# One more quarter product in six matrices, left sums kept in DRAM, a cast moved to VectorE, and pauses on GpSimd, in a relational graph layer

## The chip, the cores and the metric

One Trainium2 core of one chip. The metric is device microseconds of a whole launch; the median of three launches is given, and one further launch was profiled. TensorE is PE, VectorE is DVE, ScalarE is ACT, GpSimd is POOL and SyncE is SP, as the profile names them.

## The reference

1250 nodes with 1024 features, 20,000 edges with a source, a destination and one of 8 relations, everything in float32:

```
h   = relu(layernorm(x))
u   = h @ root + bias + sum_r mean_r(h[src], by dst) @ weight[r]
z   = concat([u, h]) @ w_gate + b_gate
out = x + tanh(u) * z + h * (1 - z)
```

`mean_r` averages over the edges of relation r that end in a node. All matrices are 1024 x 1024, and `w_gate` is two of them.

## The kernel before

**Order of the work.** The kernel multiplies first and gathers afterwards: for each of 11 matrices (s = 0 to 7 the relations, 8 the root, 9 the half of `w_gate` that takes h, 10 the half that takes u) TensorE multiplies h by the matrix. The products of the relations go to DRAM (`y`), those of matrices 8 and 9 to `hr_dram` and `z_dram`. The gather of edge rows from `y`, with a scaled addition for each (`add_slot`: GpSimd issues an indirect DMA into one of five `got` buffers, VectorE adds it to `u` with its weight), runs beside later products: those of relations 0 to 4 beside matrices 5 to 7, the rest beside matrices 8 and 9. Beside matrices 0 to 4 run the layer norm, and then an index that sorts the edges by destination: counting with one-hot matmuls, a table in DRAM that GpSimd fills by one indirect scatter for each 128 edges (`scatter`), and an order of the nodes. Matrix 10 comes last, by itself, with the gate's arithmetic.

**One product.** The 1250 rows are 10 blocks of 128, taken as 5 entries (i = 0 to 4) of two blocks (d = i and i + 5). An entry and a matrix are both cut into 2 x 2, and `product` forms them by Strassen's scheme in Winograd's form: seven products of 512 x 512 factors (`p1` to `p7`) in place of eight. `h_op[i]` holds the seven left factors (A11, A12, A22, S1 to S4), and `Factors` the seven right ones (B11, B21, B22, T1 to T4), of which VectorE makes four by `make_t1` to `make_t4`. One of the seven products is four matmuls of 512 columns for an entry; two entries need eight of them.

**Quarter products.** Entries 0 and 1, and entries 2 and 3, are taken together (`paired`). For such a pair, some of the seven products are again done by the same scheme, one level down: seven products of two matmuls of 256 columns each, in place of eight matmuls of 512 columns. There is a class for each: `First` (A11 B11), `Second` (A12 B21), `Third` (S4 B22) and `Fifth` (S1 T1). `First` and `Second` are used for matrices 1 to 9, `Third` for matrices 4 to 9 (`thirds`, `EARLY = 3`), and `Fifth` for matrices 1 to 4 (`fifths`, `FIFTHS = (1, 4)`); for matrices 5 to 9 S1 T1 is done whole, in `p5`. The sums that the quarter products need are VectorE's. `First`, `Third` and `Fifth` share one place for their sums (`room`, named `inner` in the profile), so `sums` (the factors s1, t1, s2, t2) and `next_sums` (four more in their place) have to wait until TensorE has read what lies there. `Second` has room of its own in the buffers that the matrix before has left free (named `w`): `left` and `next_left` make its four left sums from h, which are the same for every matrix, and `right` its right ones.

**What sets the order.** The schedule is written by hand: each engine does its instructions in the order in which the code gives them out. `product` calls `between(j)` after each of its parts, and `step` uses these calls to hang sums, loads and the work beside (`beside`, `sums`, `early`, `fill`) into the order. `fill` names what comes after which part. With `Fifth`, an even entry begins with `root.begin()` (a11 b11), then `first.late()`, `root.sums()`, `root.second()`, the whole product S2, `root.early()`, `root.next_sums()`, and, inside `p7`, the whole product S3, `between(TICK)` and `root.late()`. `spread` gives the steps of the gather out in proportion to a count that every `between` call raises by a number that depends on the entry.

**Memory.** PSUM has eight banks: four named `ps` in turn, two `ps_b`, one `ps_n`, one `ps_q`. `sum_bank(odd)` gives `ps_n`, or one `ps` bank that is kept for as long as `Fifth` is in use (three are then left to take turns); a matmul by `ident` writes a kept bank once before its first use. SP and ACT issue the loads and stores of matrices and rows; SP's instructions wait in their order too.

**Index.** In `slots`, each round of four times 128 edges passes `one_hots`, `count`, `add_counts`, and then splits the running counts into two bf16 parts: `as_bf16` (a cast, ScalarE) and `residue` (VectorE), which `look` multiplies.

Of the kernel before, what the change touches and what calls it, by code (L numbers as in the profile page):

```python
# [9 lines left out]
F32 = mybir.dt.float32  # L10
BF16 = mybir.dt.bfloat16
# [10 lines left out]
def tile_rgcn_highway(  # L22
# [31 lines left out]
    nc = tc.nc  # L54
# [3 lines left out]
    P = 128  # L58
# [6 lines left out]
    H = Q // 2  # L65
# [7 lines left out]
    EARLY = 3  # L73
# [5 lines left out]
    CG = 4  # L79
# [2 lines left out]
    UB = 4  # L82
    LATE = 4
    TICK = 9
    FIFTHS = (1, 4)
    IDLE = 12

# [18 lines left out]
    dram = ctx.enter_context(tc.tile_pool(name="dram", bufs=1, space=bass.MemoryType.DRAM))  # L106
# [11 lines left out]
    table = dram.tile([G * KEYS * SLOTS, 1], I32, name="table")  # L118
    table_more = dram.tile([G * KEYS * MORE, 1], I32, name="table_more")
    edges_dram = dram.tile([3, P, NCH], F32, name="edges_dram")  # L120
    val_dram = dram.tile([G, KEYS], F32, name="val_dram")
    node_dram = [dram.tile([KEYS, 1], I32, name=f"node_dram{g}") for g in range(G)]

    narrow, kept = [False], []

    def bank():
        return psum.tile([P, 512], F32, name="ps", bufs=4)

    def sum_bank(odd):

        if odd:
            if not kept:
                kept.append(bank())
                nc.tensor.matmul(kept[0].rearrange("p (c k) -> p c k", c=CG), ident,
                                 ident[:, None, :].to_broadcast([P, CG, P]), start=True, stop=True)
            return kept[0]
        return psum.tile([P, CG, P], F32, name="ps_n", bufs=1).rearrange("p c k -> p (c k)")

# [63 lines left out]
    class Second:  # L202
# [3 lines left out]
        def __init__(self, f, i):  # L206
            b = f.place["b21"]
            f0, f1 = [t.rearrange("p k n -> p (k n)") for t in f.spare]
            self.b11, self.b12, self.b21, self.b22 = [
                b[:, k:k + 2, c:c + H] for k in (0, 2) for c in (0, H)]  # L210
            self.t1, self.t2, self.t3, self.t4 = [
                f0[:, k * Q:(k + 1) * Q].rearrange("p (k n) -> p k n", k=2) for k in range(4)]
            self.s1, self.s2, self.s3, self.s4 = [
                f1[:, k * H:(k + 1) * H].rearrange("p (k n) -> p k n", k=2) for k in range(4)]
            self.p1_p6, self.p5, self.p7 = f1[:, 2 * Q:3 * Q], f1[:, 3 * Q:3 * Q + H], \
                f1[:, 3 * Q + H:]
            self.a11, self.a12, self.a21, self.a22 = [
                h_op[i + o][:, A12, k:k + 2] for o in (0, 1) for k in (0, 2)]

        def right(self, k):  # L220
            to, a, b = ((self.t1, self.b12, self.b11), (self.t2, self.b22, self.t1),
                        (self.t3, self.b22, self.b12), (self.t4, self.b21, self.t2))[k]
            nc.vector.tensor_sub(to, a, b)

        def left(self):
            nc.vector.tensor_add(self.s1, self.a21, self.a22)
# [248 lines left out]
    def product(aop, w, to, between=lambda j: None, last=None, pieces=1, whole=True,  # L475
# [38 lines left out]
        def p7():  # L514
# [3 lines left out]
            if root and head:  # L518
                between(TICK)
                root.late()  # L520
# [132 lines left out]
    fac = []  # L653
# [7 lines left out]
    def thirds(s):  # L661

        return s > EARLY
# [2 lines left out]

        return s > 0

    def fifths(s):

        return FIFTHS[0] <= s <= FIFTHS[1]

    waiting, waiting_third, waiting_first, waiting_fifth = {}, {}, {}, {}
    at_call = [0, 0]
# [9 lines left out]
    def step(s, i, between=lambda j: None, second=None):  # L684

        two = paired(s, i)
        narrow[0] = fifths(s)
        if not narrow[0]:
            kept.clear()
        if (s, i) == (NM - 2, NP - 1):  # L690
# [4 lines left out]
            t.reverse()  # L695
        if two and i % 2 == 0:
            waiting[i] = Second(fac[s], i), t[0]
            if fifths(s):
                waiting_fifth[s, i] = Fifth(fac[s], i, room, p5_room)

        def put(i, part, t):
# [11 lines left out]
        def beside(j):  # L713
            at_call[:] = i, j
            new = fac[s + 1]
            if i == 0 and s > 0 and j == 1:
                fac[s].make_t4()
            if two and i == 0:
                sums(j)
            if two and i % 2 == 0 and j == 3:  # L720
                if not root:
                    waiting_first[s, i].fifth_to()
                if i == 0:
                    waiting[0][0].left()
                if q:
                    q.sums()
            if q and i % 2 and j == 1:
                q.next_sums()
                q.first_to(to[:, Q:])
            if q and i % 2 and j == 3:  # L730
                q.fifth_to(t[0][:, Q:])
            if coming and (i > 1 or not q) and j == 2:
                first_sums()
            if two and (i, j) == (1, 6):
                Second(fac[s], 2).left()
                Second(fac[s], 2).next_left()
            if (s, i, j) == (0, 0, 3) or (s > 0 and (i, j) == (3, int(thirds(s) or fifths(s)))):
                new.load_first()
            if (s, i, j) == (0, 0, 3) or (s > 0 and (i, j) == (3, 2)):
                new.load_next()  # L740
            if i == NP - 1:
                if j == 0:
                    new.load_b22()
                elif j == 1:
                    new.make_t1()
                elif j == 3:
                    new.load_b21()
                elif j == 4:
                    new.make_t2()
                elif j == 5 and not coming:  # L750
                    new.make_t3()
                elif j == 6 and coming:
                    new.make_t3()
            between(j)

        def sums(j):


            e = waiting[0][0]
            for k in {2: (0, 1), 5: (2, 3)}.get(j, ()) if s > EARLY else (j,) if j < 4 else ():  # L760
                e.right(k)
            if j == (5 if s > EARLY else 4):
                e.next_left()

        coming = next_first(s, i)
        root = waiting_fifth.get((s, i - i % 2)) if two else None
# [11 lines left out]
        if two:  # L778
            e, to = waiting[i - i % 2]
# [73 lines left out]
    nc.tensor.matmul(sum_bank(0).rearrange("p (c k) -> p c k", c=CG), ident,  # L853
                     ident[:, None, :].to_broadcast([P, CG, P]), start=True, stop=True)
# [12 lines left out]
    apart = const.tile([P, 1], F32, name="apart")  # L867
# [76 lines left out]
    with ExitStack() as early:  # L944
# [230 lines left out]
        def scatter():  # L1175

            if placed:
                c0, c1, at, over, where = placed.pop(0)
                of = slice(c0 - at, c1 - at)
                nc.vector.scalar_tensor_tensor(at_i[:, c0:c1], over[:, of], float(FAR),  # L1180
                                               where[:, of], op0=OP.mult, op1=OP.add)
                for c in range(c0, c1):
                    n = nedges(c)
                    ins = nc.gpsimd.indirect_dma_start(  # L1184
                        out=table[:, :],
                        out_offset=bass.IndirectOffsetOnAxis(ap=at_i[:n, c:c + 1], axis=0),
                        in_=row_col[:n, c:c + 1], in_offset=None,
                        bounds_check=G * KEYS * SLOTS - 1, oob_is_err=False)
                    tc.declare_no_dep(ins.ins, query=no_wait, group="scatter", reason="each edge has its own slot")
                    tc.add_to_no_dep_group("scatter", ins.ins)  # L1190

        def slots(ix):

# [3 lines left out]
            seen = ix.tile([P, RING, NHI], F32, name="seen", bufs=1)  # L1197
# [290 lines left out]
        while going[0]:  # L1488
            s, i = next(steps)
# [11 lines left out]
    with ExitStack() as edges_part:  # L1501
# [89 lines left out]
        def spread(e, total, parts):  # L1591

            said = [0, 0]
            parts *= 10

            def between(j):
                said[0] += (10, 8, 13, 11, 8)[at_call[0]]
                while said[1] < min(total, -(-total * said[0] // parts)):
                    next(e, None)
                    said[1] += 1  # L1600
                if said[0] == parts:
                    for _ in e:
                        pass

            return between
# [45 lines left out]
        s, i = next(steps)  # L1651
        while s <= EARLY:
            step(s, i)
            s, i = next(steps)
# [90 lines left out]
        while s < R0[1]:  # L1745
            step(s, i, on)
            s, i = next(steps)
# [14 lines left out]
        s, i = beside(first_group, sum(K[0]) + LATE + 1, s, i, R0[2] - 1)  # L1762
# [4 lines left out]
        with tc.If(passes > 0):  # L1767
# [15 lines left out]
            p = Passes()  # L1783
# [125 lines left out]
        while s < NM - 1:  # L1909
# [8 lines left out]
            s, i = next(steps, (NM, 0))  # L1918
# [86 lines left out]
```

## Time and profile before

| | before |
|---|---|
| time of three launches, us | 1330.55, 1331.38, 1331.61 (median 1331.38) |
| the profiled launch, us | 1331.68 |
| its span in the profile, us | 1329.9 |
| PE, DVE, ACT, POOL busy, us | 1315.0, 1028.2, 279.5, 579.2 |
| DMA moved | 263.75 MB, mean 198 GB/s |

The span is what the profile covers; the launch's time is 1.8 us more. Busy time is a sum over the instructions of an engine. A float32 matmul shows as two records in the trace, so that a group of four matmuls has the count x8. A row of the chain of waits gives a start, a length and what ran.

### The profile page before, as it was taken

Reading aid. Unit: us, or ns where it says so; the run is one execution under the profiler, and the core shown is the slowest. Engines: PE = TensorE matmul, PEld = TensorE weight load, DVE = VectorE, ACT = ScalarE, POOL = GpSimd, SP = SyncE. Lnnn points to the kernel's source line nnn. Section 1 sums busy time; section 2 is a strip of 40 time slices with the busy share of each in tenths; the row PEclk is TensorE's granted clock in tenths of the full one; section 3 lists DMA queues with packets and bytes.
Section 4 is the critical chain, followed back from the end, with each engine's and each line's share of the span. In section 5 each row is a group of like instructions: output and inputs, shape, how many; then the busy total and the mean of one; then the engine's idle time right before and its main releaser. Section 6 shows DMA issues by size and latency. Waiting matters only on the chain.

```text
span 1329.9 us, 13668 instructions
## 1 busy us (share of the span) xinstructions
PE 1315.0 (99%) x4212; PEld 734.2 (55%) x4212; DVE 1028.2 (77%) x2132; ACT 279.5 (21%) x547; POOL 579.2 (44%) x510
## 2 busy tenths in 40 slices
PE   9999999999999999999999999999999999999997
PEld 5444565556455546655655655565465556544443
DVE  6768977797784676558977988897788799867974
ACT  3352122122112212211221211121122112122210
POOL 0001546454655047401453546446265555715631
PEclk9999999999999999999999999999999999999999
DMA  8976355734834252144648769778788957969961
GB/s 306 302 228 165 87 96 129 155 60 77 161 103 101 81 115 49 53 159 153 221 138 305 254 236 368 261 256 275 250 280 304 353 180 246 323 249 292 326 178 60
DMA packets 116802, 263.75 MB, mean 198 GB/s; under 512 B 33150, under 2 KB 44818, under 8 KB 116592
## 3 DMA queue, kind: packets, MB, share of 16 engines
q1 hardware_dynamic: 56528, 112.62, 28.4%
q0 software_dynamic: 44064, 118.20, 28.1%
q10 hardware_dynamic: 16128, 31.98, 7.9%
q8 instruction: 33, 0.54, 0.2%
q14 instruction: 49, 0.40, 0.1%
HBM read 202.34 MB, written 75.41 MB: 209 GB/s over the span
## 4 chain that ended last, share of the span: by engine, by line
PE 81%; issue 6%; DMA 5%; DVE 5%; POOL 2%; SPq 1%; ACT 1%; POOLq 0%; DVEq 0%
PE ps_b L491 39%; PE ps L235 16%; PE ps L491 11%; PE ps_n L491 5%; PE ps_b L235 3%; PE ps_n L235 2%; DMA got<-y,idx 2%; PE ps_q L235 2%; PE ps_q L491 2%; DMA xt<-in_x_dram 1%; POOL got L1533 1%; DMA w<-in_L_gnn_weight_dram 1%; DVE u L1538 1%; POOL out_dram L878 0%; DVE h_op L472 0%
## 5 line engine op out<-in xcount | busy, mean ns | idle before, releaser
L491 PE MATMUL ps_b<-w,h_op 128*128 128x512 f32 x1464 | 659.1, 594 | 1.0 <-ACT row L595 0.8
L491 PEld LDWEIGHTS ps_b<-w,h_op 128*128 128x128 f32 x1464 | 274.4, 190 | 305.0 <-issue 294.2
L1533 POOL DMA_INDIRECT got<-y,idx x193 | 248.2, 1286 | 285.9 <-DVE u L1538 184.1
L1538 DVE SCALAR_TENSOR_TENSOR u<-got,w_of,u 128x1024 f32<-128x1024 f32 (+1 forms) x193 | 246.8, 1281 | 40.6 <-DMA got<-y,idx 38.1
L1184 POOL DMA_INDIRECT table<-row_col,at_i x157 | 172.6, 1099 | 154.6 <-DVE at_i L1180 109.0
L491 PE MATMUL ps<-w,h_op 128*128 128x512 f32 (+1 forms) x432 | 192.1, 586 | 0.8 <-ACT row L569 0.8
L491 PEld LDWEIGHTS ps<-w,h_op 128*128 128x128 f32 x432 | 81.1, 190 | 91.5 <-issue 85.9
L491 PE MATMUL ps_n<-w,h_op 128*128 128x512 f32 x208 | 94.4, 593 | 0.0
L235 PE MATMUL ps<-inner 128*128 128x256 f32 x360 | 91.6, 380 | 0.3 <-DVE inner L290 0.3
L235 PE MATMUL ps<-w,h_op 128*128 128x256 f32 x320 | 83.0, 382 | 1.0 <-ACT w L252 1.0
L235 PEld LDWEIGHTS ps<-inner 128*128 128x128 f32 x360 | 67.8, 190 | 18.6 <-issue 9.0
L517 ACT COPY row<-ps_b 128x512 f32<-128x512 f32 x53 | 31.0, 585 | 218.2 <-PE ps_b L491 218.2
L235 PEld LDWEIGHTS ps<-w,h_op 128*128 128x128 f32 x320 | 59.9, 190 | 28.8 <-issue 20.2
L595 ACT COPY row<-ps_b 128x512 f32<-128x512 f32 x54 | 31.6, 585 | 205.1 <-PE ps_b L491 205.1
L235 PE MATMUL ps<-w,w 128*128 128x256 f32 x288 | 70.8, 380 | 0.5 <-ACT w L241 0.5
L235 PEld LDWEIGHTS ps<-w,w 128*128 128x128 f32 x288 | 54.3, 190 | 20.1 <-issue 13.4
L491 PEld LDWEIGHTS ps_n<-w,h_op 128*128 128x128 f32 x208 | 39.3, 190 | 45.1 <-issue 44.2
L523 DVE TENSOR_TENSOR row<-row 128x512 f32<-128x512 f32 x44 | 30.2, 686 | 44.0 <-ACT row L517 42.5
L639 ACT COPY row<-ps_b 128x512 f32<-128x512 f32 x40 | 23.4, 585 | 175.8 <-PE ps_b L491 142.7
L1299 DVE SCALAR_TENSOR_TENSOR junk<-k_bc,key_col,before 128x128 f32<-128x128 int16 x157 | 54.8, 349 | 4.2
L552 ACT COPY row<-ps_b 128x512 f32<-128x512 f32 x54 | 31.7, 587 | 83.5 <-PE ps_b L491 76.1
L448 POOL MEMSET h_op<- 32x1024 f32 x1 | 0.9, 946 | 97.1 <-DVE rs L986 97.1
(254 smaller groups left out, 1539.9 us busy)
## 6 DMA issues: line engine op xcount, KB each, us to landing
y<-row SPq DMA_DIRECT2D x72, 512.0 KB
w<-in_L_gnn_weight_dram ACTq DMA_DIRECT2D x21, 1024.0 KB
w<-in_L_gnn_weight_dram SPq DMA_DIRECT2D x10, 1024.0 KB
w<-in_L_gnn_w_gate_dram ACTq DMA_DIRECT2D x6, 1024.0 KB
k_bc<-keys_dram SPq DMA_DIRECT2D x39, 128.0 KB
l_bc<-los_dram SPq DMA_DIRECT2D x39, 128.0 KB
h_dram<-h_op SPq DMA_DIRECT2D x9, 512.0 KB
u<-in_L_gnn_bias_dram SPq DMA_DIRECT2D x9, 512.0 KB
```

The lines of the kernel that those rows point to most:

```text
L235: nc.tensor.matmul(p, a[:, k, :], b[:, k, :], start=(fresh and k == 0), stop=(k == 1), skip_group_check=True)
L448: nc.gpsimd.memset(to[n // 32 * 32:], 0.0)
L491: nc.tensor.matmul(b[:, at], aop[:, i, k, :], w.of[i][:, k, at], start=(fresh and k == 0), stop=(k == KQ - 1), skip_group_check=True)
L517: nc.scalar.copy(d, b)
L523: nc.vector.tensor_add(c22, c if lone else c22, d)
L552: nc.scalar.copy(c11, b)
L595: nc.scalar.copy(c12, b)
L639: nc.scalar.copy(c21, b)
L1184: ins = nc.gpsimd.indirect_dma_start(out=table[:, :], out_offset=bass.IndirectOffsetOnAxis(ap=at_i[:n, c:c + 1], axis=0), in_=row_col[:n, ...
L1299: nc.vector.scalar_tensor_tensor(junk, o["k_bc"][:, i, :], key_col[:, c:c + 1], before, op0=OP.is_equal, op1=OP.mult, accum_out=rank[:, c: ...
L1533: nc.gpsimd.indirect_dma_start(out=t[:n], out_offset=None, in_=y[g][:, :], in_offset=bass.IndirectOffsetOnAxis(ap=at[:n, d, k:k + 1], axis=0),
L1538: nc.vector.scalar_tensor_tensor(u[:n], t[:n], w, u[:n], op0=OP.mult, op1=OP.add)
```

## The change

- `fifths(s, i)` is true for every matrix from 1 on, so `Fifth` is used in matrices 5 to 9 as well. The whole product S1 T1 of entries 0 to 3 goes in these, and the kept `ps` bank stays kept up to the end of matrix 9.
- The left sums of `Second` are made in matrix 1 alone, and stored to `lefts_dram` (one DMA of 512 KB for each pair of entries). From matrix 2 on SP loads them: for entries 0 and 1 at `(0, 0)`, for entries 2 and 3 at `(1, 6)`.
- `as_bf16` is a `tensor_copy` of VectorE in place of a copy of ScalarE.
- After each scatter into the table GpSimd does three memsets of one column (`apart`).
- `touch`, which writes a kept bank first, reads the identity as bf16, and stands ahead of eleven small matmuls at the start (before: eight small ones, then a float32 one).
- `spread` doesn't count the `TICK` call of entries other than 0, so that its sum stays what it was.

```diff
-    FIFTHS = (1, 4)
+    LEFTS_AT = 6
...
+    def touch(b):
+        of = ident.bitcast(BF16)[:, :P]
+        nc.tensor.matmul(b.rearrange("p (c k) -> p c k", c=CG), of,
+                         of[:, None, :].to_broadcast([P, CG, P]), start=True, stop=True)
...
-                nc.tensor.matmul(kept[0].rearrange("p (c k) -> p c k", c=CG), ident,
-                                 ident[:, None, :].to_broadcast([P, CG, P]), start=True, stop=True)
+                touch(kept[0])
...
+        def keep_lefts(self):
+            s, of = self.lefts()
+            nc.sync.dma_start(of, s)
+
+        def load_lefts(self):
+            s, of = self.lefts()
+            nc.sync.dma_start(s, of)
...
-    def fifths(s):
-        return FIFTHS[0] <= s <= FIFTHS[1]
+    def fifths(s, i=0):
+        return s > 0
...
-                if i == 0:
+                if i == 0 and s == 1:
                     waiting[0][0].left()
...
-            if two and (i, j) == (1, 6):
+            if two and (i, j) == (1, 6) and s == 1:
                 Second(fac[s], 2).left()
                 Second(fac[s], 2).next_left()
+                Second(fac[s], 2).keep_lefts()
+            if two and s > 1 and (i, j) == (0, 0):
+                waiting[0][0].load_lefts()
+            if two and s > 1 and (i, j) == (1, LEFTS_AT):
+                Second(fac[s], 2).load_lefts()
...
-            if j == (5 if s > EARLY else 4):
+            if s == 1 and j == 4:
                 e.next_left()
+                e.keep_lefts()
...
-    for _ in range(IDLE - CG):
+    touch(sum_bank(0))
+    for _ in range(IDLE - 1):
         nc.tensor.matmul(bank()[:, :P], ident, ident, start=True, stop=True)
...
                     tc.add_to_no_dep_group("scatter", ins.ins)
+                    for _ in range(3):
+                        nc.gpsimd.memset(apart, 0.0)
...
-                        nc.scalar.copy(s_b[:, to:to + n, 0], seen[:, k:k + n])
+                        nc.vector.tensor_copy(s_b[:, to:to + n, 0], seen[:, k:k + n])
...
-                said[0] += (10, 8, 13, 11, 8)[at_call[0]]
+                if j != TICK or at_call[0] == 0:
+                    said[0] += (10, 8, 13, 11, 8)[at_call[0]]
```

More of the change, by code (lines that the diff above doesn't have):

```diff
@@ L120, in tile_rgcn_highway @@
     edges_dram = dram.tile([3, P, NCH], F32, name="edges_dram")
+    lefts_dram = dram.tile([2, P, 4 * H], F32, name="lefts_dram")
     val_dram = dram.tile([G, KEYS], F32, name="val_dram")
@@ L214, in __init__ @@
                 f1[:, k * H:(k + 1) * H].rearrange("p (k n) -> p k n", k=2) for k in range(4)]
+            self.i, self.s_all = i, f1[:, :4 * H]
             self.p1_p6, self.p5, self.p7 = f1[:, 2 * Q:3 * Q], f1[:, 3 * Q:3 * Q + H], \
@@ L223, in right, with lefts @@
             nc.vector.tensor_sub(to, a, b)
+        def lefts(self):
+            return self.s_all, lefts_dram[self.i // 2]
+        def keep_lefts(self):
[4 more added lines that the diff above has]
+            nc.sync.dma_start(s, of)
         def left(self):
@@ L686, in step @@
         two = paired(s, i)
-        narrow[0] = fifths(s)
+        narrow[0] = fifths(s, i)
         if not narrow[0]:
@@ L697, in step @@
             waiting[i] = Second(fac[s], i), t[0]
-            if fifths(s):
+            if fifths(s, i):
                 waiting_fifth[s, i] = Fifth(fac[s], i, room, p5_room)
@@ L849, in tile_rgcn_highway @@
     make_identity(nc, ident)
-    for _ in range(IDLE - CG):
+    touch(sum_bank(0))
+    for _ in range(IDLE - 1):
         nc.tensor.matmul(bank()[:, :P], ident, ident, start=True, stop=True)
-    nc.tensor.matmul(sum_bank(0).rearrange("p (c k) -> p c k", c=CG), ident,
-                     ident[:, None, :].to_broadcast([P, CG, P]), start=True, stop=True)
     eps = const.tile([P, 1], F32, name="eps")
```

## The prediction

> **What bounds the kernel now.** I read the totals of the page first, then the table of stages, then TensorE's waits, then VectorE's waits stage by stage, and last the chain of waits. The totals (engine, busy us, share):
>
> ```profile
> PE 1315.0 (99%) x4212; PEld 734.2 (55%) x4212; DVE 1028.2 (77%) x2132; ACT 279.5 (21%) x547; POOL 579.2 (44%) x510
> ```
>
> A busy PE can hide waits, so I look for them stage by stage. Each row is one stretch: its bounds, its length, then busy us of PE, PEld, DVE, ACT, POOL, the granted clock, and the DMA share. I cut them near the matrices' borders; the rows are matrices 2, 4, 5, 7 and 8.
>
> ```profile
> 266.00:388.00 122.00, 121.25 (x475) 69.95 (x475) 97.80 (x390) 25.02 (x65) 69.74 (x61) 1.00 0.53 108
> ...
> 505.00:614.00 109.00, 109.00 (x357) 66.89 (x356) 67.21 (x145) 21.71 (x45) 32.91 (x31) 1.00 0.26 80
> 614.00:730.00 116.00, 116.00 (x354) 66.39 (x353) 98.00 (x153) 20.82 (x42) 53.34 (x44) 1.00 0.66 225
> ...
> 846.00:962.00 116.00, 115.65 (x352) 66.11 (x352) 95.18 (x121) 20.82 (x42) 53.92 (x46) 1.00 0.78 263
> 962.00:1078.00 116.00, 116.00 (x353) 66.38 (x352) 96.10 (x128) 20.83 (x42) 66.60 (x52) 1.00 0.88 307
> ```
>
> PE fills every stage at clock 1.00. VectorE has 18 to 21 us free in each of matrices 5 to 9, and 42 us in matrix 4, which already has the layout that matrices 5 to 9 are to get. TensorE's own waits (us in total, times, longest):
>
> ```profile
> PE ps L235 <- ACT w L252: 1.0, 3, 0.5
> ...
> PE ps L491 <- ACT row L569: 0.8, 2, 0.5
> ...
> PE ps L235 <- ACT w L241: 0.5, 1, 0.5
> PE ps L235 <- DVE inner L290: 0.3, 1, 0.3
> ```
>
> All waits of PE together are under 7 us in 1330. So the time is TensorE's work, and only less work, or a new wait, can move it. That is what the change has to be weighed by. VectorE's largest wait in matrices 7 and 8, one row from each stage's list:
>
> ```profile
> DVE u L1538 <- DMA got<-y,idx: 12.3, 7, 3.1
> DVE u L1538 <- DMA got<-y,idx: 12.1, 11, 2.0
> ```
>
> There VectorE stands for a gathered row while later instructions of its queue wait behind, among them the sums that TensorE needs.
>
> **TensorE's work.** The price of a group of matmuls is read from the chain of waits, in matrix 3 (start, us, what):
>
> ```profile
> 407.51 3.45 PE ps L235 x16
> ...
> 469.65 6.87 PE ps_b L491 x16
> ```
>
> Sixteen records of 512 columns take 6.87 us: that is one whole product for two entries. Sixteen records of 256 columns take 3.45 us, 0.216 each. The quarter form has 14 matmuls, 28 records: 28 x 0.216 = 6.04. The gain is 0.83 us for a pair of entries. The order of instructions of the changed kernel agrees: 80 matmuls of 512 columns are gone and 140 of 256 have come, for ten pairs (two in each of matrices 5 to 9). **-8.3 us**, all of it on the path.
>
> The kept bank's first write moves from float32 to bf16. The row `ps<-ident 128x512` has two records in matrix 1, where PE is full: 2 x 0.43 = 0.86. The bf16 form is one record; no bf16 matmul of 512 columns is in the trace, but those of 80 and 20 columns last 196 and 171 ns, 0.42 ns a column, so 0.21 us. **-0.65 us.** At the start the same change, and three more small matmuls, lie in a time in which PE waits for the first transposes anyway (they start at 7.83, after `h_op` of VectorE): 0, between -0.2 and +0.5 if the idle stretch of 1.6 us before 7.83 should let the clock fall. The Trainium skill (TensorE: Matmul & The Clock Gate, Part 1) puts the idle time that lowers the clock at about 3.4 us, which would leave it up; no row here shows a fall, and the sum takes 0.
>
> **VectorE's work.** One `Fifth` pair adds four sums of 256 columns (0.42 us each), four of 512 (0.68) and two additions into PSUM (0.43): 5.3 us by durations, 4.6 by starts, since neighbours overlap. Two pairs: +9 to +10.5 for a matrix. Gone are eight left sums of 0.42: -3.3. Net +6 to +7 in matrices 5 to 9, so 103 of 114 us are busy; in matrices 2 to 4 it is only -3.3. Free time of VectorE costs nothing and busy time costs nothing as long as the sums are early enough, so I count the queue at the tight places. From matrix 4: sums of `room` start 0.25 us after TensorE has issued its last read, four take 1.9.
>
> Entry 0, from T, the end of `first.late()`: VectorE does `root.sums()` (to T+2.15), `fifth_to` (2.55), two gather additions of 1.28 (5.1), `make_t4` 2.29 (7.4), one more gather addition (8.7), the addition into `ps_n` (9.1), and the first two of `next_sums` (10.1). TensorE does `second` 0.86, S2 3.43, `early` 1.73, the A12 B21 part 0.86, S3 3.43, and wants them at T+10.3. Early by 0.2. Entry 2: three gather additions and no `make_t4`, so T+7.8 against T+9.45, early by 1.65. This is how it stands in matrices 5 to 7. In matrix 8 entry 0 has no gather addition there, entry 2 has four (early by 0.4). In matrix 9 entry 0 has one ahead of the sums (late by about 0.5), and entry 2 has four and an addition of `hr` rows, 1.22 (late by 0.85). **+1.4 us.** What is queued behind such a late sum is only VectorE's own next work; who waits is TensorE.
>
> Gathers that land late come on top. The waits of 12 us a matrix come where five buffers are used up in a row, and the new order has runs of seven and eight gather additions behind the second entry's sums (six before). Those have slack: after such a run VectorE frees a PSUM bank about 2.5 us before TensorE takes it. Late landings at the tight places cost between 0 and the longest wait, 3.1, at each of four or five places in matrices 7 to 9; but VectorE comes later to each gather than before, by 6 us a matrix, which takes up part of the same waits. I take **+1.0**, with 0 and 14 as ends.
>
> **The cast.** 53 casts leave ScalarE (26 of 0.26, 13 of 0.24, 14 of 0.21 us, 12.8 in all) and join VectorE. The nearest rows there are the `residue` subtractions of the same shapes, 232, 216 and 171 ns: 11.2 us over 39 rounds between 86 and 400 us, where VectorE has about 24 us free in a matrix and gets 4 more work. Upper end +1 if a cast delays sums (the tightest place there is early by 1.2), and I take 0. ScalarE gains: its casts wait 5.7 us for `residue` and hold back two PSUM copies behind them, at 277.5 and 287.9, for which PE stands 0.8 us. **-0.5.** The Trainium skill (DMA: Bandwidth & Descriptors, SWDGE vs HWDGE vs iDMA) says that VectorE in its two-port mode locks GpSimd out of the SBUF state in which it writes descriptors, and a float32 copy from SBUF to SBUF is a candidate for it. It speaks against this step; by it the scatters would lose at most the casts' own 11 us, and no run here shows it yet.
>
> **GpSimd.** 157 x 3 memsets of 0.09 to 0.17 us (rows `eps` and `apart`) are 42 to 80 us more. The scatters' group was idle 155 us before its instructions, 109 of it waiting for VectorE's addresses, and the first gather waited 59.9 us for the bias rows, so that the cover is there: 0. If it were gone, the order's last 8 us would move to the gathers' start.
>
> **Left sums by DMA.** SP gets two stores and 16 loads of 512 KB, 9.4 MB on 264, at `(0, 0)` and `(1, 6)`. On SP they stand between row stores; what queues behind is the next row store, for which nobody waits. The second load is the nearer: TensorE uses it about 15 us after its place, and the first x rows landed in 4.3 us among eight other loads. 0; if SP were held by a row store (its longest waits are above 25 us), up to 10 us once.
>
> **Sum** against the profiled launch: 1331.68 - 8.3 - 0.65 - 0.5 + 1.4 + 1.0 = 1324.6. The runs' median lies 0.3 under that launch: **1324.3**.
>
> **Rivals.** (a) VectorE becomes the bound in matrices 7 to 9: 95.2 busy, 12.3 waiting for gathers and 7 more make 114.5 of 114 us. If each gather wait stays, the sums come late at every head of a pair: with 1.5 us at each of ten pairs and 1 in the other tight place of each it is +25 - 8.95, about 1347; at 0.9 us a pair it is level. For it: VectorE's queue is in order, and entry 0 has 0.2 us of slack. Against it: before, with 12 us of such waits, TensorE stood 0.3 us for a sum. From 1.2 us a pair on it is slower: 1334 to 1347. (b) Half comes: late sums also in matrices 5 and 6 and late gathers cost 3 to 6 us: 1327.5 to 1331. (c) Nothing changes, because one `ps` bank fewer makes each pair wait about 0.6 us (a copy by ScalarE, 585 ns) where a bank turns over: 10 x 0.6 and the waits above, 1330 to 1332. Matrix 4, PE 109.00 of 109.00 with that bank kept, speaks against it. That the quarter form isn't used is excluded by the order.
>
> **Numbers.** My forecast's own range is 1321 (no new wait, ScalarE's waits gone) to 1327.5, with 0.68; (b) 0.15, (c) 0.06, (a) 0.11. The range from 1321.2 to 1331.0 leaves out (a) and the edges. A difference under 0.2%, 2.7 us, can hardly be told from none: faster takes the forecast and half of (b), 0.76; same takes the other half and (c), 0.13; slower takes (a), 0.11.
>
> **What would show it.** Right: matrices 5 to 9 take some 114.2 us each in place of 115.9, PE full, VectorE near 103; the list of PE's waits gets a few rows `ps<-inner` on VectorE's sums, in matrices 8 and 9, of 1 to 3 us in all; the two ScalarE waits of matrix 2 are gone. Wrong: waits of PE on sums of over 8 us, or rows in which PE waits for the loaded left sums or for a `ps` bank; or matrices 1 and 2 longer than before, which would put the cast on the path.

## The result, and the profile after

The changed kernel takes 1336.73 us (median of five launches, 1333.59 to 1338.05); the kernel before, beside it on the same chip, 1331.37. The ratio is 1.0040, with a 95% interval of 1.0027 to 1.0053: slower by 0.4%, where 1324.3 was forecast with a range of 1321.2 to 1331.0. Three more comparisons, on three chips, gave 1.0036, 1.0042 and 1.0035.

One thing is needed to read the numbers below: on two of the chips that the experiments ran on, the kernel before takes 1348.5 us in place of 1330.7. Each run is therefore given with the kernel before on its own chip.

The profiled launch took 1336.73 us, with a span of 1334.9. Its totals:

```profile
PE 1309.6 (98%) x4336; PEld 759.0 (57%) x4336; DVE 1054.5 (79%) x2221; ACT 283.7 (21%) x524; POOL 647.3 (48%) x981
```

PE has 5.4 us less work than before (1315.0) and a span 5.0 us longer. The time went into waits. TensorE's list of waits (us in total, times, longest):

```profile
PE ps L255 <- DVE row L283: 6.7, 3, 2.5
PE ps L511 <- DVE row L352: 3.3, 1, 3.3
...
PE ps L255 <- DVE inner L310: 1.0, 1, 1.0
...
PE ps L255 <- DVE inner L316: 0.6, 1, 0.6
```

(L255 and L511 are the matmuls of a quarter and of a whole product, L235 and L491 before.) The two last rows are late sums, 1.6 us together, as the prediction expected them, though one of them is in matrix 7 (L310) and one in matrix 9 (L316). The two first it did not have: VectorE's addition L283, the second half of `Second.to_first`, frees the bank `ps` that `e.second` needs next, and L352, in `Third.last_to`, frees the kept bank that the S1 product of the lone entry (entry 4) needs. A list counts a wait from the end of the matmul before it, as the profile models that end. Counted from start to start a stall is 0.2 us longer (2.6 for the 2.45 in matrix 6 below), and stalls named in the text are counted so. The stages (matrices 2, 4, 5 to 9 nearly; bounds, length, then busy us of PE, PEld, DVE, ACT, POOL, clock and DMA share):

```profile
266.00:388.00 122.00, 121.74 (x477) 70.33 (x476) 98.10 (x402) 21.84 (x44) 80.22 (x211) 1.00 0.54 118
505.00:614.00 109.00, 109.00 (x360) 67.34 (x359) 64.00 (x136) 21.79 (x46) 36.81 (x37) 1.00 0.36 92
614.00:730.00 116.00, 116.00 (x387) 72.38 (x386) 105.53 (x166) 24.27 (x51) 56.14 (x44) 1.00 0.69 237
730.00:846.00 116.00, 113.55 (x375) 70.54 (x374) 102.32 (x137) 22.79 (x48) 60.55 (x49) 1.00 0.83 288
846.00:962.00 116.00, 114.97 (x380) 71.10 (x379) 102.72 (x136) 23.47 (x50) 59.31 (x46) 1.00 0.81 274
962.00:1078.00 116.00, 110.71 (x359) 68.19 (x359) 98.37 (x136) 22.30 (x46) 64.21 (x51) 0.99 0.89 314
1078.00:1194.00 116.00, 112.47 (x372) 69.30 (x372) 95.89 (x129) 26.30 (x50) 58.78 (x43) 0.99 0.77 252
```

Up to matrix 5 PE is full, as forecast, or within 0.3 us of it. From matrix 6 on 1.0 to 5.3 us are missing in each stretch of 116. Gathers run in matrix 5 too, at a DMA share of 0.69; from matrix 6 on it is 0.77 to 0.89. Matrix 6 shows how the time is lost; a stretch of the timeline (start, us, engine, line, operation, idle before it and what ended that):

```profile
790.75 6.56 DVE L1565 SCALAR_TENSOR_TENSOR u<-got,w_of,u 128x1024 f32<-128x1024 f32 x5
...
794.51 1.02 POOL L1560 DMA_INDIRECT got<-y,idx  x1 [0.30 <-issue]
...
798.35 1.28 DVE L1565 SCALAR_TENSOR_TENSOR u<-got,w_of,u 128x1024 f32<-128x1024 f32 x1 [1.04 <-DMA got<-y,idx]
...
799.73 3.60 PE L511 MATMUL ps_b<-w,h_op 128*128 128x512 f32 x8
...
803.32 1.28 DVE L1565 SCALAR_TENSOR_TENSOR u<-got,w_of,u 128x1024 f32<-128x1024 f32 x1 [3.69 <-DMA got<-y,idx]
...
804.52 0.68 DVE L282 TENSOR_TENSOR row<-row,w 128x512 f32<-128x512 f32 x1
...
805.31 0.42 DVE L283 TENSOR_TENSOR row<-row,ps 128x256 f32<-128x256 f32 x1
...
805.78 1.13 PE L255 MATMUL ps<-w,h_op 128*128 128x256 f32 x4 [2.45 <-DVE row L283]
```

Five additions find their rows in the five buffers. The sixth and the seventh use the buffers that the first and the second have just freed; the seventh's gather was issued at 794.51 and lands at 803.3. L282 and L283 stand behind it in VectorE's queue, and TensorE, done with its whole product at 803.3, stands until L283 has read the bank. The chain of waits of the same launch has that landing as a step of its own:

```profile
794.51 8.71 DMA got<-y,idx
806.91 3.43 PE ps_b L511 x8
```

In the kernel before, the same place of matrix 6 had only three gather additions ahead of L262 and L263, and the bank was free at 798.5:

```profile
793.44 3.92 DVE L1538 SCALAR_TENSOR_TENSOR u<-got,w_of,u 128x1024 f32<-128x1024 f32 x3
...
798.07 0.42 DVE L263 TENSOR_TENSOR row<-row,ps 128x256 f32<-128x256 f32 x1
```

The row alone is not enough. In matrix 5 of the changed kernel seven gather additions stand ahead of L283 too; there VectorE stood 1.5 us for a landing, L283 ended at 688.4, and TensorE, which came at 689.0, did not wait. Nor do landings take longer than before (median 6.0 us in matrices 5 to 9, before 6.1), and VectorE's waits for them add up to 33.7 us, before to 38.1. What is new is where they fall.

### The profile page after: what moved, and what is told of

Its sections match the earlier page's. It is cut to its first block, busy times and chain, and to the rows that moved or that the text cites. A ratio compares the mean times of both kernels' runs of the same rounds, so it can differ in the third digit from the quotient of the medians.

```text
span 1334.9 us, 14558 instructions
## 1 busy us (share of the span) xinstructions
PE 1309.6 (98%) x4336; PEld 759.0 (57%) x4336; DVE 1054.5 (79%) x2221; ACT 283.7 (21%) x524; POOL 647.3 (48%) x981
## 4 chain that ended last, share of the span: by engine, by line
PE 64%; DVE 12%; issue 10%; DMA 9%; POOL 3%; SPq 1%; ACT 1%; POOLq 0%; DVEq 0%
PE ps_b L511 30%; PE ps L255 14%; PE ps L511 9%; DMA got<-y,idx 6%; DVE u L1565 3%; PE ps_b L255 3%; PE ps_n L255 2%; PE ps_n L511 2%; POOL got L1560 1%; PE ps_q L511 1%; DMA xt<-in_x_dram 1%; PE ps_q L255 1%; DMA h_op<-z_dram,node 1%; DMA w<-in_L_gnn_weight_dram 1%; POOL out_dram L903 1%
## 5 line engine op out<-in xcount | busy, mean ns | idle before, releaser
L511 PE MATMUL ps_b<-w,h_op 128*128 128x512 f32 x1464 | 658.6, 594 | 1.0 <-ACT row L615 0.8
L511 PEld LDWEIGHTS ps_b<-w,h_op 128*128 128x128 f32 x1464 | 276.5, 190 | 298.3 <-issue 290.9
L1560 POOL DMA_INDIRECT got<-y,idx x193 | 255.9, 1326 | 277.4 <-DVE u L1565 187.2
L1565 DVE SCALAR_TENSOR_TENSOR u<-got,w_of,u 128x1024 f32<-128x1024 f32 (+1 forms) x193 | 246.8, 1281 | 36.4 <-DMA got<-y,idx 33.7
L1209 POOL DMA_INDIRECT table<-row_col,at_i x157 | 183.8, 1171 | 119.4 <-issue 85.0
L511 PE MATMUL ps<-w,h_op 128*128 128x512 f32 (+1 forms) x352 | 157.7, 590 | 4.4 <-DVE row L352 3.3
L255 PE MATMUL ps<-inner 128*128 128x256 f32 x480 | 120.9, 380 | 1.6 <-DVE inner L310 1.0
L511 PEld LDWEIGHTS ps<-w,h_op 128*128 128x128 f32 x352 | 66.3, 192 | 81.8 <-issue 71.0
L255 PEld LDWEIGHTS ps<-inner 128*128 128x128 f32 x480 | 90.5, 190 | 27.1 <-issue 10.8
L255 PE MATMUL ps<-w,h_op 128*128 128x256 f32 x360 | 94.4, 385 | 7.7 <-DVE row L283 6.7
L255 PEld LDWEIGHTS ps<-w,h_op 128*128 128x128 f32 x360 | 67.5, 191 | 40.2 <-issue 20.9
L255 PE MATMUL ps<-w,w 128*128 128x256 f32 x288 | 69.7, 380 | 0.0
L1217 POOL MEMSET apart<- 128x1 f32 x471 | 54.4, 115 | 18.1
L255 PEld LDWEIGHTS ps<-w,w 128*128 128x128 f32 x288 | 54.4, 190 | 15.0 <-issue 8.6
L511 PE MATMUL ps_n<-w,h_op 128*128 128x512 f32 x128 | 57.6, 593 | 0.0
```

The costliest lines, as they stand in the source:

```text
L255: nc.tensor.matmul(p, a[:, k, :], b[:, k, :], start=(fresh and k == 0), stop=(k == 1), skip_group_check=True)
L511: nc.tensor.matmul(b[:, at], aop[:, i, k, :], w.of[i][:, k, at], start=(fresh and k == 0), stop=(k == KQ - 1), skip_group_check=True)
L1209: ins = nc.gpsimd.indirect_dma_start(out=table[:, :], out_offset=bass.IndirectOffsetOnAxis(ap=at_i[:n, c:c + 1], axis=0), in_=row_col[:n, ...
L1217: nc.gpsimd.memset(apart, 0.0)
L1560: nc.gpsimd.indirect_dma_start(out=t[:n], out_offset=None, in_=y[g][:, :], in_offset=bass.IndirectOffsetOnAxis(ap=at[:n, d, k:k + 1], axis=0),
L1565: nc.vector.scalar_tensor_tensor(u[:n], t[:n], w, u[:n], op0=OP.mult, op1=OP.add)
```

## The experiments

Three theories stood against each other. **Late bank**: the new order puts seven or eight gather additions in a row ahead of an addition that frees a PSUM bank, five buffers can't cover them, and the landings reach TensorE. **Load**: VectorE simply has too much to do (rival (a) of the prediction). **Other parts**: the loads of the left sums, the cast or the fillers (the memsets on GpSimd) cost the time.

To compare runs on chips that differ before matrix 5, this table shows the start of the last entry in matrices 5 to 9 and the end (the last matmul), against the first trace of the kernel before, as changes since the same point of matrix 4 (us, worked out from the traces; negative is faster):

| kernel | 5 | 6 | 7 | 8 | 9 | end |
|---|---|---|---|---|---|---|
| changed | -1.7 | -0.8 | -2.4 | -1.3 | +6.9 | +6.9 |
| no_gathers | -1.7 | -3.5 | -5.2 | -7.6 | -8.5 | -8.5 |
| quarters_to_4 | 0.0 | 0.0 | 0.0 | +0.9 | +0.9 | +0.9 |
| bank_add_early | -1.7 | -3.5 | -2.8 | -3.4 | +2.6 | +4.5 |
| spread_moved | -1.7 | -3.5 | -5.2 | -7.6 | -0.9 | -0.3 |
| spread_both | -1.7 | -3.5 | -5.2 | -7.6 | -4.2 | -4.2 |
| both_moves | -1.7 | -3.5 | -5.2 | -7.6 | -4.6 | -4.6 |
| both_moves_again | -1.7 | -3.5 | -5.2 | -7.6 | -2.6 | -2.6 |
| quarters_alone | -1.0 | -0.1 | -0.3 | +0.6 | +10.8 | +11.2 |

**The landings, or VectorE's load: no_gathers.**

```
-            t = got()
-            nc.gpsimd.indirect_dma_start(out=t[:n], in_=y[g][:, :], ...)
+            t = still
...
```

> The changed kernel with the 193 gathers left out: each addition multiplies and adds one still tile of zeros in place of the gathered rows, so VectorE does the same additions in the same order and never waits for a landing (the sums of the edges are missing). Theory 'late bank': VectorE no longer stops inside the rows, L283 and L352 come 2 to 4 us earlier, TensorE's waits for them and the lower clock behind (8.4 and 4.9 us) go: 1320 to 1325 us. Theory 'load': VectorE is as busy as before, so TensorE waits as before: 1333 to 1338 us.

Measured 1326.29 us, the kernel before 1348.51 on that chip. One of the five buffers makes room for `still`, and the sums of the edges are left out. VectorE still has its 193 additions and 1053.8 us of work, but no longer stops for a landing, and PE is full in the stages:

```profile
L1563 DVE SCALAR_TENSOR_TENSOR u<-still,w_of,u 128x1024 f32<-128x1024 f32 (+1 forms) x193 | 246.4, 1281 | 3.1
```

```profile
614.00:730.00 116.00, 116.00 (x387) 72.50 (x386) 105.18 (x167) 23.59 (x49) 1.12 (x2) 1.00 0.29 104
846.00:962.00 116.00, 116.00 (x384) 72.12 (x383) 103.51 (x141) 23.23 (x48) 10.55 (x11) 1.00 0.38 134
962.00:1078.00 116.00, 116.00 (x382) 71.89 (x381) 103.40 (x138) 23.23 (x48) 11.03 (x8) 1.00 0.45 153
```

The first is the group of the additions (last number: idle us before them, 36.4 in the changed kernel); the others are matrix 5, 7 and 8. VectorE is as busy as with gathers, PE loses nothing, and TensorE's list has no row for L283 or L352. 'Load' falls. The time itself lies 1.3 us above the expected range; the profiled launch has a stall of 1.4 us in matrix 4 that the changed kernel's first trace does not have.

**Undoing the quarters: quarters_to_4.**

```
     def fifths(s, i=0):
-        return s > 0
+        return 0 < s <= 4
```

> The changed kernel with the quarter products in matrices 1 to 4 only, as before the change; the bf16 touches, VectorE's cast, GpSimd's fillers, and the left sums by DRAM all stay. Theory 'late bank': in matrices 5 to 9 the quarters put seven or eight gather additions in a row ahead of the addition that frees e.c's PSUM bank (L283), and TensorE waits for it. Without the quarters those rows of additions are split again, so the loss of 15.8 us and the gain of 8.7 us both go: what is left is the -1.71 us that the trace shows at the start of matrix 4's last entry, 1331.4 - 1.7 = 1329.7 us (1329 to 1331.5). Theory 'load': VectorE is 90% busy beside the gather additions and any order would do; the same time here, so it is not told apart. Theory 'other parts': the loads of the left sums, or the fillers on GpSimd, hold up the gathers: the loss stays, 1334 us or more.

Measured 1333.65 us, the kernel before 1348.67. The expected time was for a chip on which the kernel before takes 1331 us; what can be read is the table: from matrix 4 on the kernel runs level with the one before, within 0.9 us. Gain and loss are both the quarters'. The loads of the left sums are still there and cost nothing.

**The quarters alone: quarters_alone.**

```
 (kernel before)
     def fifths(s):
-        return FIFTHS[0] <= s <= FIFTHS[1]
+        return s > 0
 ... and the rule on TICK in spread
```

> The kernel before with the quarter products in matrices 5 to 9 alone (and the rule that leaves the count of gather steps as it was): no bf16 touch, no cast on VectorE, no fillers, and the left sums formed again by VectorE in each matrix, some 1.3 us of work more than with the load. Theory 'late bank': the rows of seven and eight gather additions are there, and L283 comes later by VectorE's extra work: the changed kernel's loss without its gains elsewhere, 1336 to 1342 us where the kernel before takes 1330.7. Theory 'other parts' (loads of the left sums delay gathers): without those loads no loss, 1322 to 1325 us.

Measured 1361.92 us, the kernel before 1348.51: slower by 13.4, without any of the other parts, where 5.3 to 11.3 were expected. From matrix 4 on it loses 11.2 us, more than the changed kernel. 'Other parts' falls as a cause of the loss. TensorE waits for the same two additions (L263 and L332 by this kernel's lines), and besides for left sums (L231), which VectorE makes here in each matrix:

```profile
PE ps L235 <- DVE row L263: 5.2, 3, 2.1
PE ps L235 <- DVE w L231: 4.8, 4, 1.9
...
PE ps L491 <- DVE row L332: 3.6, 2, 3.3
```

**Moving one addition: bank_add_early.**

```
-    fourth=lambda: (e.sixth(), True))
+    fourth=lambda: (e.sixth(), e.free_bank(to), True))   # free_bank is L283
...
```

> The changed kernel with one addition moved in VectorE's order: the one that frees e.c's bank (L283) is issued right after e.sixth, one call of the gather stream earlier, so that some five gather additions stand ahead of it in place of seven or eight; the amount of work is the same on every engine. Theory 'late bank': TensorE's waits for L283 (2.62 us in matrix 6, 2.18 in 8, 2.41 in 9, and about 1.7 us of lower clock behind the last) go, the wait for the kept bank in matrix 8 (3.43 us and about 1.4 of lower clock) stays or moves a little: 1336.7 - 8.9 = 1327.8 us (1326 to 1330). Theory 'load': the same work on the same engine, so 1335 to 1338 us. Theory 'other parts': 1335 to 1338 us.

Measured 1341.93 us, the kernel before 1348.67. The time says little, since the changed kernel did not run on that chip, but the mechanism is half what was expected: no wait for L283 is left, and the one for L352 (L357 by this kernel's lines) has grown:

```profile
PE ps L516 <- DVE row L357: 8.3, 3, 5.1
```

It seems that the gathers for which VectorE no longer waits ahead of L283 make it wait a little later, ahead of L352: the expectation took a moved wait for a removed one. Its 8.9 us were 2.4 in the table.

**Shorter rows: spread_moved, spread_both, both_moves.** These change the weights by which `spread` gives out gather steps; both_moves issues L283 early as well.

```
-                if j != TICK or at_call[0] == 0:
+                if at_call[0] == 2:
+                    said[0] += {0: 18, 1: 20, 2: 18, TICK: 0, 6: 8}.get(j, 9)
+                elif at_call[0] == 3:                # not in spread_moved
+                    said[0] += {3: 6, 4: 6, 5: 16, 6: 16}.get(j, 11)
+                elif j != TICK or at_call[0] == 0:
                     said[0] += (10, 8, 13, 11, 8)[at_call[0]]
```

> The changed kernel with the gather steps of entry 2 spread otherwise: the same sum over the entry, but 18, 20, 18 for its first three calls and 9, 9, 9, 8 for its last four, in place of 13 each, so that five gather additions stand ahead of L282 and L283 in place of seven, and five in place of three stand ahead of the sum to0 (L434) in the same entry, where VectorE idles 2.3 us of the time in the changed kernel's trace. Theory 'late bank': the waits for L283 go, as five buffers are full when the row of five begins: 1327.8 us if L434 is in time; up to 1.3 us in each of five matrices if it is not, 1327 to 1333 us. Theory 'load': 1335 to 1338 us.

Measured 1332.46 us, the kernel before 1348.67. Five additions stand ahead of L283, and its waits are gone; up to matrix 8 the kernel follows no_gathers to 0.1 us. What is left is L352 in matrix 8, and late sums in matrix 9:

```profile
PE ps L511 <- DVE row L352: 3.6, 2, 3.3
PE ps L255 <- DVE inner L316: 2.7, 2, 2.1
```

> The changed kernel with the gather steps of entry 2 spread as in the run of that name (five or six additions ahead of L283 in place of seven or eight), and those of entry 3 too: the same sum of 77, but 6 in place of 11 for its fourth and fifth call and 16 for its last two, so that one or two gather additions fewer stand ahead of the addition that frees the kept bank (L352). Theory 'late bank': no wait for L283, and the wait for L352 in matrix 8 (3.43 us and about 2 us of lower clock in the run with entry 2 alone) shrinks to under 1: with the kernel before at 1330.7, its -1.7 of matrices 1 and 2 and -1.74 in each of five matrices, some 2 us of smaller stalls: 1322 to 1327 us. Theory 'load': the same work on VectorE in another order, 1334 to 1338 us.

Measured 1330.06 us, the kernel before 1348.51: 3 us above the upper end. The wait for L352 is gone, as expected; the longer row ahead of `to0` now makes `next_sums` late (L316: 4.3 us in three waits), and matrix 4, where no gather runs, has two stalls of 2.2 us.

> The kernel of the run before (gather steps of entries 2 and 3 spread otherwise) with L283 also issued right after e.sixth: four or five gather additions ahead of it. Theory 'late bank': five buffers already cover a row of five, so nothing more is won: within 2 us of the run before, 1321 to 1327 us. Theory 'load': 1334 to 1338 us.

Measured 1327.46 us beside 1348.51, half a us above the range. Its own change, L283 early, adds nothing that can be told apart, as expected: the two kernels agree in their waits for sums (4.0 and 4.3 us), and differ by the stalls in matrix 4.

> The version with the gather steps of entries 2 and 3 spread otherwise and L283 issued right after e.sixth. Theory 'late bank': 1323 to 1328 us on either kind of chip; it beats the kernel before by 0.3 to 0.6% where that takes 1331 us, and the changed kernel by 9 us or more.

The same kernel on a chip where the kernel before takes 1330.63 us: **1325.71 us, ratio 0.9956 (0.9942 to 0.9969)**. It beats both kernels. The profiled launch:

```profile
PE 1306.3 (99%) x4336; PEld 758.3 (57%) x4336; DVE 1054.1 (80%) x2221; ACT 283.8 (21%) x524; POOL 650.9 (49%) x981
```

```profile
PE ps L255 <- DVE inner L321: 4.4, 3, 2.3
```

VectorE's work and TensorE's are those of the changed kernel; on that chip the order alone makes 10.3 us (1335.96 less 1325.71). The remaining wait is for the second sum of `next_sums`, the tight place the prediction had counted, with more gather additions ahead of it.

**The parts priced at nothing.** In fillers_only and fillers_again, the kernel before gets the three memsets after each scatter; in cast_only and cast_again the cast on VectorE.

> The kernel before with one part of the change, the three small memsets on GpSimd after each table scatter. If back-to-back scatters cost the 17 us: 1331 to 1334 us where the kernel before takes 1348. If the cast on ScalarE does, 1348. Where the kernel before takes 1331, 1331 to 1332: the prediction had priced the part at nothing.

> The kernel before with one part of the change, the counts' cast on VectorE. If back-to-back scatters cost the 17 us, 1347 to 1349 us where the kernel before takes 1348; if the cast on ScalarE does, 1331 to 1334. Where the kernel before takes 1331, 1330.5 to 1331.5: the prediction had priced the part at -0.5 us.

The kernel before took 1330.65 us there. Fillers: 1330.21 us, 0.9996 (0.9987 to 1.0005). Cast: 1329.59 us, 0.9991 (0.9982 to 1.0000), a gain of 1.1 where 0.5 was expected. The table scatters, in which GpSimd could have been locked out by VectorE's copies, lasted as long (kernel before on that chip, then with the cast):

```profile
L1184 POOL DMA_INDIRECT table<-row_col,at_i x157 | 172.5, 1099 | 154.7 <-DVE at_i L1180 109.1 <-issue 37.6 <-DVE own L1286 4.5
```

```profile
L1184 POOL DMA_INDIRECT table<-row_col,at_i x157 | 174.9, 1114 | 150.4 <-DVE at_i L1180 99.1 <-issue 38.6 <-DVE s_b L1257 11.8
```

15 ns a scatter more, 2.4 us in all, and hidden.

**What the chip with 1348 us shows: cast_by_act.**

```
-                    for _ in range(3):
-                        nc.gpsimd.memset(apart, 0.0)
...
-                        nc.vector.tensor_copy(s_b[:, to:to + n, 0], seen[:, k:k + n])
+                        nc.scalar.copy(s_b[:, to:to + n, 0], seen[:, k:k + n])
```

> The changed kernel with the two index-stage parts undone: the counts' cast on ScalarE again, and no fillers on GpSimd between table scatters. Theory 'late bank': both are off the path that sets the end; -0.5 us of the trace at matrix 2 may go back: 1336.2 to 1338 us. Theory 'other parts': if they cost what was lost, 1331.5 us or less.

Measured 1361.89 in the profiled launch, 1362.22 in the median, the kernel before 1348.67: neither theory had a place for a loss. It has 26.9 us more than the kernel before's first trace by the last entry of matrix 4, in stalls like this one in matrix 1:

```profile
172.31 0.98 POOL L1209 DMA_INDIRECT table<-row_col,at_i  x1 [0.30 <-issue]
173.59 0.98 POOL L1209 DMA_INDIRECT table<-row_col,at_i  x1 [0.30 <-issue]
174.88 0.98 POOL L1209 DMA_INDIRECT table<-row_col,at_i  x1 [0.30 <-issue]
176.16 0.98 POOL L1209 DMA_INDIRECT table<-row_col,at_i  x1 [0.30 <-issue]
178.99 0.58 ACT L615 COPY row<-ps_b 128x512 f32<-128x512 f32 x1 [6.71 <-remote]
179.08 0.33 DVE L1311 TENSOR_TENSOR own<-ps_q,is_at 128x160 f32<-128x160 f32 x1 [7.05 <-remote]
...
179.62 1.22 PE L511 MATMUL ps_b<-w,h_op 128*128 128x512 f32 x1 [5.38 <-ACT row L615]
```

ScalarE, VectorE and then TensorE stand for 5 to 7 us, though the products that the first two wait for had ended by 173.3, while GpSimd issues scatter after scatter with 0.30 us between. The runs on the same two chips that have fillers and the cast on VectorE have no such stall in matrices 1 to 3 (in matrix 4 they have one or two each, of 1.4 to 6.1 us, which were not traced to anything); quarters_alone, which has neither, has stalls of 2.7, 3.3 and 4.6 us there.

> The kernel before, for its trace on this chip. Theory 'chip': if its time is near 1348 us, TensorE has stalls of 2 to 6 us in matrices 1 to 4 (100 to 590 us) that the first trace does not have, each beside a row of table scatters 0.30 us apart, and from matrix 5 on the marks run as in the first trace; if it is near 1331 us, none. Theory 'chance': the 17 us are spread over the whole span.

> The kernel before with the fillers alone. On a chip where the kernel before takes 1348 us: 1331 to 1335 us if scatters issued back to back are what holds TensorE up there; 1348 if the cast on ScalarE is. Where the kernel before takes 1331 us: 1330 to 1331, as run before.

> The kernel before with the cast on VectorE alone. On a chip where the kernel before takes 1348 us: 1345 to 1349 us if scatters issued back to back are the cause; 1331 to 1335 if the cast on ScalarE is. Where the kernel before takes 1331 us: 1329 to 1330.5, as run before.

> The kernel before with the fillers alone. On a chip where the kernel before takes 1348 us: 1331 to 1335 us if scatters issued back to back are what holds TensorE up there, 1348 if the cast on ScalarE is. Where it takes 1331 us: 1330 to 1330.5, as run before.

These four met chips on which the kernel before takes 1330.7 us: 1330.34 us for the kernel before, with no stall above 0.65 us from matrix 1 to 8; 1330.09 and 1330.01 with fillers, beside 1330.63 and 1330.72; 1329.53 with the cast, beside 1330.63.

> The changed kernel as it is, beside the kernel before on the same chip. In the last runs the kernel before took 1348.7 us, 17 more than at first, and the changed kernel with its two index-stage parts undone lost 26 us in matrices 1 to 4 (its two longest stalls of TensorE 5.5 and 5.0 us, while GpSimd issued table scatters 0.30 us apart). Theory 'chip': chips differ in what back-to-back scatters cost; where the kernel before takes 1348, the changed kernel takes 1337 to 1344 us and is the faster one, where it takes 1331 the changed kernel takes 1334 to 1338 and is the slower one. Theory 'chance': the first comparison was off; the changed kernel is slower by 0.4% on any chip, 1354 beside 1348.7.

> The changed kernel as it is. On a chip where the kernel before takes 1348 us: 1336 to 1342 us, some 0.7% faster, since it has the fillers and the cast and loses 7 to 14 us behind the gather landings as on the first chip. On a chip where the kernel before takes 1331 us: 1334 to 1338 us, 0.4% slower.

> The changed kernel as it is. On a chip where the kernel before takes 1348 us: 1336 to 1344 us, 0.3 to 0.9% faster. On a chip where it takes 1331 us: 1335 to 1336.5 us, as run before.

So did the changed kernel: 1335.30, 1335.96 and 1334.88 us beside 1330.65, 1330.63 and 1330.72. What it takes on a chip where the kernel before takes 1348 us stays open, and so does which of its two index-stage parts takes those stalls away.

## Why the prediction was wrong

**Right.** The quarter product is worth what was worked out: forecast -8.3 us in five matrices, -8.5 in no_gathers, where almost nothing covers it. The touch of the kept bank: forecast -0.65, measured -0.62 between the last entries of matrices 0 and 1 (-0.14 and -0.76 against the kernel before). The cast off ScalarE: forecast -0.5; the stretch up to matrix 2's last entry gained 0.95, and cast_only 1.1. Fillers, loads of the left sums and the start at 0: fillers_only 0.4 (within its interval), no row of TensorE for the loads, and -0.14 at matrix 0's last entry, where two traces of the kernel before differ by 0.76. VectorE has 95.9 to 105.5 us of work in the stretches of matrices 5 to 9, where 103 of 114 were forecast. Late sums in matrix 9: forecast +1.4, measured 0.8 in the changed kernel.

**Wrong: one step.** "Those have slack: after such a run VectorE frees a PSUM bank about 2.5 us before TensorE takes it." The prediction saw the runs of seven and eight additions and the five buffers, and took the slack at the end of the run for larger than the waits for landings in it. But the run itself makes the landings late: its sixth and seventh gather can only be issued once the first and second addition are over, and a landing takes long (last row of the list for the tile `got`, matrices 5 to 9):

```profile
DMA to landing us min/median/max: 2.1/6.0/13.2
```

VectorE stood 4.7 us in the row of matrix 6, used up the 2.5 us and passed the rest on. The term **+1.0** for late gathers measured, in the first trace: 2.6, 2.2 and 2.4 us for L283 in matrices 6, 8 and 9, 3.4 for L352 in 8, 1.2 for a late sum in 7, and some 3.1 lost at half the clock behind two of them, 15 us in all. The stated upper end of 14 was about right, but the range left it out; only rival (a), at 0.11, reached that far. Among its own signs of being wrong the prediction had named the one that came, rows in which PE waits for a `ps` bank.

**The rivals.** The time lies in the range of (a), but not for its reason: VectorE is not the bound (no_gathers), and late sums, where (a) put the loss, are 1.6 us of TensorE's list against 10.0 for the two additions. (c) named the `ps` bank, but had a copy by ScalarE hold it, for 0.6 us a pair, where it is an addition by VectorE behind late gathers. That one bank fewer in turn is why TensorE needs this bank so soon is argued from the code: no run had the quarters with four banks in turn. Matrix 4, which spoke against (c), has the bank kept and no gathers, so it could not show the two together.

## What to carry to other kernels

Slack behind a row of uses is not to be counted as if the data had landed: when a new order puts more uses of a ring in a row than the ring has buffers, a use past the last buffer waits for a transfer that can be issued only inside the row. Here issue to landing takes 6 to 9 us for 512 KB, of which VectorE stood 1.0 and 3.7 us in matrix 6, and everything queued behind stands too. A stage that is the model for a change (matrix 4 here) speaks only for the resources that are in use there. When such waits appear, spreading the uses costs no memory (more buffers were not tried); look at the next release behind the one that was mended: moving L283 alone sent the wait on to L352.

## What the runs showed of the hardware

**The clock.** In the first trace of the changed kernel the granted clock fell behind the waits of matrices 8 and 9, and not behind that of matrix 6 (stretches of 10 us, columns as above, the clock next to the last two):

```profile
800.00:810.00 10.00, 7.55 (x20) 3.53 (x19) 6.44 (x13) 0.58 (x1) 2.68 (x3) 1.00 0.99 354
...
1050.00:1060.00 10.00, 6.73 (x13) 2.78 (x12) 7.27 (x9) 0.58 (x1) 4.64 (x4) 0.83 1.03 407
...
1160.00:1170.00 10.00, 10.00 (x28) 6.11 (x29) 9.79 (x16) 0.59 (x1) 5.04 (x5) 0.83 0.96 340
```

The stalls were 2.6, 3.4 and 2.4 us. In the repeats, stalls of 2.4, 2.5, 2.7, 2.8 and 3.5 us were followed by one to six records of 512 columns at 0.85 us or more in place of 0.43, and others of 2.3, 2.4, 3.3 and 3.6 us by none. The Trainium skill (TensorE: Matmul & The Clock Gate, Part 1) puts the idle time that lowers the clock at about 3.4 us, in a window that runs freely. These runs show falls from 2.4 us on, and that the length alone does not decide. What does is how a stall lies to a fixed grid. In each trace the granted clock changes only at points of a grid with steps of 3.413 us: in the first it is at half from 1054.31 to 1057.73 and from 1160.13 to 1163.54, and the two falls are 31 such steps apart. Cut at these points, from matrix 1 to 9 of all twenty traces, the 20 stretches that a fall followed had 2.04 to 3.41 us in which TensorE stood, and every other stretch at full clock had at most 1.91. The stall of matrix 6 is cut into 1.81 and 0.64 us, and no fall followed. So a window that runs freely agrees with these traces, but 2.04 us of standing inside one was enough.

**Chips.** The same kernel before takes 1330.6 to 1330.7 us on three chips (medians), 1331.4 at first, and 1348.5 and 1348.7 on two others. Each of these two was met once, so that the chip and the time of the run can't be told apart. Kernels without fillers and cast show stalls of up to 5.5 us in matrices 1 to 4 on these two; the one printed above ends within 0.7 us on three engines. Whether the spacing of the scatters or the cast takes them away was not shown.
